# Layer 3's inverse square roots computed on VectorE and GpSimd instead of ScalarE

## The chip, the core and the metric

The kernel runs on one core of one Trainium2 chip. A core has five engines with a queue of instructions each: TensorE (PE, with its weight loads shown as PEld), VectorE (DVE), ScalarE (ACT), GpSimd (POOL) and SyncE (SP, which here only issues transfers). The metric is the device time of one execution in microseconds (us).

## The reference

Four layers follow each other on x of 4 batches x 256 tokens x 256 features, each an attention over a context of 1601 rows and a feed-forward part (ffn), both added to x after a layer norm. The change lies in layer 3:

```python
# L3 attention: 32 heads of 8 dims, 256 queries, 1601 keys per batch
q = x @ Wq.T                      # x: layer-normed tokens, eps 1e-5
k_raw = context @ Wk.T;  v_raw = context @ Wv.T
kv = concat([k_raw, v_raw]).reshape(b, m, NHEADS, HEAD_DIM, 2)   # k, v interleaved
def _rmsnorm(t): return t * rsqrt(mean(t * t, axis=-1) + 1e-6)   # over the 8 dims
q = _rmsnorm(q);  k = _rmsnorm(k)
out = softmax(einsum('bhnd,bhmd->bhnm', q, k) * HEAD_DIM ** -0.5) @ v
x = x + out
# L3 ffn: silu(gate) * up, then down, with activations rounded to 8 bits by their row maximum
x = x + ffn(layernorm(x))
```

Three kinds of inverse square root occur: per key and head (1601 x 32 a batch), per query and head (256 x 32 a batch), and per token (256 a batch) in the two layer norms.

## The kernel before

The program is written in a tile framework: a scheduler fixes the order of instructions on each engine ahead of the run, an engine's queue is worked off strictly in that order, and a tile's buffer is given to its next user when the last reader of the old one is done. Tokens, and keys in tiles of 128 rows (13 tiles, NM = 13), lie on the 128 partitions.

**Keys.** The generator l3_kv(b) makes the keys and values of batch b, one key tile m at a time: a product with the weights wkv into a PSUM bank, one copy to kr (L1683) and two to va (L1685). After m = 4, 9 and 12, l3_squares squares the new tiles into the tile sq3 (one buffer; ScalarE at L1721 where `early()` is true, else GpSimd at L1723) and VectorE sums over the 8 dims into ss (L1724). kr is then multiplied by the inverse roots in ss on GpSimd (L1701, four instructions), transposed on TensorE (L1712), and copied to kT (L1713). Batch 0's keys are made inside layer 2's ffn, where their root is rstd: a Sqrt on ScalarE (L81) and a reciprocal on VectorE (L82). 11 of batch 1's 13 key tiles are made as filling inside queries(0), the list FIRST3 = [7, 1, 3] saying how many at each place; the rest, and batches 2 and 3, beside the attention of the batch before.

**Queries.** queries(b) normalises x (xn, L1767), transposes it (L1797), copies it to xT (L1799), multiplies by wq, copies to qr (L1807), squares (ScalarE) into sqq and sums (L1724), takes the root, multiplies (L1813), transposes (L1824) and copies to qT (L1825). For b > 0 a single Sqrt over 128x482 (L1810) covers the keys (416 columns), the queries (64) and two columns for the token norm of batch b - 2, which the ffn of that batch will use; VectorE's reciprocals follow (L1811 for 66 columns, L1816 twice for 208).

**Norms.** norms(bs) takes mean and variance (L1761, L1762: st, mv) and rstd of the variance into rs.

**Attention.** For every batch 8 groups of heads, and in each 7 pairs of key tiles: scores (s, L77), the exponential on ScalarE (e, L1943), the product with the values (o, L77), where three score tiles (ps_s) may be in flight, and one step of a side generator, beside(b):

```python
for _ in range(NM - 3 if b else NM - sum(FIRST3)):
    next(kv)                       # keys of batch b + 1
    yield
qs = queries(b + 1, st, b - 1 if b else None)
for _ in range(2):
    next(qs)
    yield
for _ in kv: yield                 # multiply, transpose the keys
for _ in qs: yield                 # transpose the queries
...                                # then the ffn of batch b - 1
```

Every side step takes its PSUM bank from bank(), tile b3, of which there is one buffer: the next product into it waits for the copies out of it. After a group of heads os is copied (L2040) and closed (L1960 to L1970: transposed, divided, added to x on GpSimd). spread (L1923) makes the masked queries qb of the next group. The exponential, the Sqrt and the ffn's tanh use different tables of ScalarE; each change of table is an instruction ACT_TABLE_LOAD, shown at the line of the activation that needs it.

Of the kernel before, what the change touches and what calls it, by code (L numbers as in the profile page):

```python
# [11 lines left out]
F32 = mybir.dt.float32  # L12
# [4 lines left out]
I32 = mybir.dt.int32  # L17
AF = mybir.ActivationFunctionType
ALU = mybir.AluOpType
# [39 lines left out]
class Kernel:  # L59
# [19 lines left out]
    def rstd(self, out, in_, scale, eps):  # L79

        self.nc.scalar.activation(out, in_, AF.Sqrt, bias=eps, scale=scale)  # L81
        self.nc.vector.reciprocal(out, out)  # L82

    def layernorm(self, out, x):

# [1582 lines left out]
    def l3_kv(self, b, st, early):  # L1668


        nc = self.nc
        ctxT = self.ctx3
        pool = self.late3 if b % 2 else self.a3
        kr = st["kr"] = self.a3.tile([P, NM, D], F32, name="kr3")
        va = st["va"] = self.va3[b % 2]
        ss = st["ss"] = self.a3.tile([P, (NM + 2) * NH3 + 2], F32, name="ss3")
        for m in range(NM):
            copy = nc.scalar.copy if early() else nc.vector.tensor_copy
            tf = self.take()
            for k in range(2):  # L1680
                self.mm(tf, ctxT[:, k, m * P : (m + 1) * P], self.wkv3[:, k, :], k == 0, k == 1)
            tp = tf.rearrange("p (h d c) -> p h d c", d=HD3, c=2)
            copy(kr[:, m, :].rearrange("p (h d) -> p h d", d=HD3), tp[:, :, :, 0])  # L1683
            for h in range(2):
                copy(  # L1685
                    va[h][:, m, : 16 * (HD3 + 1)].rearrange("p (h e) -> p h e", e=HD3 + 1)[:, :, :HD3],
                    tp[:, h * 16 : (h + 1) * 16, :, 1],
                )
            if m in (4, 9, NM - 1):
                m0 = {4: 0, 9: 5}.get(m, 10)  # L1690
                self.l3_squares(st, kr[:, m0 : m + 1, :], m0, early())
            if m == NM - 1 and b < B - 1:
                self.ctx3 = self.load_ctxT(self.a3, b + 1, 1)
            yield
        if b == 0:
            nk = NM * NH3
            self.rstd(ss[:, :nk], ss[:, :nk], 1.0 / HD3, self.eps6)
        for m0, m1 in ((0, 4), (4, 8), (8, 12), (12, NM)):
            v = kr[:, m0:m1, :].rearrange("p m (h d) -> p (m h) d", d=HD3)
            f = ss[:, m0 * NH3 : m1 * NH3, None].to_broadcast([P, (m1 - m0) * NH3, HD3])  # L1700
            nc.gpsimd.tensor_tensor(v, v, f, ALU.mult)  # L1701
        yield
        yield
        yield
        kT = st["kT"] = [pool.tile([P, MP], F32, name="kT3", bufs=2) for _ in range(2)]
        for m0 in range(0, NM, 4):
            for h in range(2):
                n = min(4, NM - m0)
                copy = nc.scalar.copy if early() else nc.vector.tensor_copy
                tp = self.take().rearrange("p (m k) -> p m k", k=P)  # L1710
                for m in range(n):
                    nc.tensor.transpose(tp[:, m, :], kr[:, m0 + m, h * P : (h + 1) * P], self.ident)  # L1712
                copy(kT[h][:, m0 * P : (m0 + n) * P], tp[:, :n, :].rearrange("p m k -> p (m k)"))  # L1713
                yield

    def l3_squares(self, st, v, m0, early, pool=None):

        n = v.shape[1]
        sq = (pool or self.a3).tile([P, 2 if pool else 5, D], F32, name="sqq3" if pool else "sq3")
        if early:  # L1720
            self.nc.scalar.activation(sq[:, :n, :], v, AF.Square)  # L1721
        else:
            self.nc.gpsimd.tensor_tensor(sq[:, :n, :], v, v, ALU.mult)  # L1723
        self.nc.vector.tensor_reduce(  # L1724
            st["ss"][:, m0 * NH3 : (m0 + n) * NH3], sq[:, :n, :].rearrange("p m (h d) -> p (m h) d", d=HD3),
            AX.X, ALU.add,
        )

    def l3(self, first):

# [10 lines left out]
        with ExitStack() as es:  # L1741
# [30 lines left out]
            def norms(bs):  # L1772

                for b in bs:
                    stats(b)
                v = slice(bs[0], bs[-1] + 1)
                self.rstd(rs[:, v, :], mv[:, v, :, 1], 1.0, self.eps5)

            def queries(b, st, old=None, fill=lambda n: None):

                ss = st["ss"]
                nk, nq = NM * NH3, (NM + 2) * NH3
                if old is not None:
                    stats(old)
                    nc.vector.tensor_scalar(
                        ss[:, nq:], mv[:, old, :, 1], float(HD3), HD3 * (1e-5 - 1e-6), ALU.mult, ALU.add
                    )
                elif b:  # L1790
                    nc.vector.memset(ss[:, nq:], 1.0)
                xn = normed(b, rs[:, b, :])
                fill(0)
                tp = bank().rearrange("p (k q t) -> p k q t", k=2, q=2)
                for k in range(2):
                    for q in range(2):
                        nc.tensor.transpose(tp[:, k, q, :], xn[:, q, k * P : (k + 1) * P], self.ident)  # L1797
                xT = one.tile([P, 2, S], F32, name="xT3")
                nc.vector.tensor_copy(xT, tp.rearrange("p k q t -> p k (q t)"))  # L1799
                fill(1)  # L1800
                yield
                tq = bank().rearrange("p (q d) -> p q d", q=2)
                for q in range(2):
                    for k in range(2):
                        self.mm(tq[:, q, :], xT[:, k, q * P : (q + 1) * P], self.wq3[:, k, :], k == 0, k == 1)
                qr = one.tile([P, 2, D], F32, name="qr3")
                nc.vector.tensor_copy(qr, tq)  # L1807
                self.l3_squares(st, qr, NM, True, one)
                part = ss if b else ss[:, nk:nq]
                nc.scalar.activation(part, part, AF.Sqrt, bias=self.eps6, scale=1.0 / HD3)  # L1810
                nc.vector.reciprocal(ss[:, nk : nq + 2 if b else nq], ss[:, nk : nq + 2 if b else nq])  # L1811
                qrv = qr.rearrange("p q (h d) -> p (q h) d", d=HD3)
                nc.vector.tensor_tensor(qrv, qrv, ss[:, nk:nq, None].to_broadcast([P, 2 * NH3, HD3]), ALU.mult)  # L1813
                if b:
                    for c in range(0, nk, nk // 2):
                        nc.vector.reciprocal(ss[:, c : c + nk // 2], ss[:, c : c + nk // 2])  # L1816
                fill(2)
                yield
                yield
                qT = st["qT"] = two.tile([P, 2, S], F32, name="qT3")  # L1820
                tp = bank().rearrange("p (h t) -> p h t", h=2)
                for h in range(2):
                    for q in range(2):
                        nc.tensor.transpose(tp[:, h, q * P : (q + 1) * P], qr[:, q, h * P : (h + 1) * P], self.ident)  # L1824
                nc.vector.tensor_copy(qT, tp)  # L1825
                yield
# [145 lines left out]
            def beside(b, st):  # L1972

                if b + 1 < B:
                    kv = st["kv"] if b == 0 else self.l3_kv(b + 1, st, lambda: False)
                    if b:
                        for _ in range(3):
                            next(kv)
                            yield
                    if b == 0:  # L1980
                        norms(range(1, B))
                    for _ in range(NM - 3 if b else NM - sum(FIRST3)):
                        next(kv)
                        yield
                    qs = queries(b + 1, st, b - 1 if b else None)
                    for _ in range(2):
                        next(qs)
                        yield
                    for _ in kv:
                        yield  # L1990
                    for _ in qs:
                        yield
                    nq = (NM + 2) * NH3
                    old = [normed(b - 1, st["ss"][:, nq:])] if b else []
                else:
                    for _ in range(3):
                        yield
                    norms([b - 1])
                    old = [normed(b - 1, rs[:, b - 1, :])]
# [12 lines left out]
            kv = second["kv"] = self.l3_kv(1, second, lambda: not busy)  # L2012
            self.l2_add(0)
            norms([0])
            for _ in queries(0, first, None, lambda n: [next(kv) for _ in range(FIRST3[n])]):
                pass
            busy = True
            self.take = bank
# [40 lines left out]
                    :, : 512 if dt is F32 else 1024  # L2059
                ]  # L2060

            norms([B - 1])
            xn = normed(B - 1, rs[:, B - 1, :])
            tail = [ffn(B - 1, q, xn, wide) for q in range(2)]
            while tail:
# [161 lines left out]
```

## Time and profile before

| | |
|---|---|
| median of 6 runs | 2567.95 us (2560.74 to 2572.91) |
| the profiled execution's own time | 2570.77 us |
| its span in the trace | 2568.8 us |
| busy share: TensorE, VectorE, ScalarE, GpSimd | 95%, 55%, 51%, 33% |
| instructions: TensorE, VectorE, ScalarE, GpSimd | 17623, 2915, 3000, 1516 |
| layer 2's ffn and the start of layer 3 | about 1735 to 1941 us |
| attention of batches 0, 1, 2, 3 | 1941 to 2102, to 2265, to 2430, to 2540 us |
| last ffn | 2540 to 2569 us |

All rows come from one profiled execution, so the sums of the prediction start from its own time. A row such as "L1943 ACT ACTIVATE e<-s ... x448 | 404.5, 960 | 159.3 <-PE s L77 154.3" gives line, engine, operation, output and input, count, then busy us and mean ns of one, then the engine's idle time before these and what ended most of it. In a timeline the first two numbers are the start and the length in us; brackets give the idle time ahead and what ended it.

### The profile page before, as it was taken

The page shows a single profiled execution, that of the slowest core. Times are in us where ns is not written, and L with a number is a line of the kernel's source. Part 1 is how long each engine was busy: PE and PEld are TensorE (multiplying, and loading weights), DVE is VectorE, ACT ScalarE, POOL GpSimd, SP SyncE. Part 2 cuts the span into 40 slices and gives each one's busy share as a digit, 9 for nine tenths or more (in the row PEclk, how much of TensorE's full clock was granted, in tenths as well). Part 3 has the DMA queues.
Part 4 walks back from the last instruction along what each step waited for, and adds up shares of the span by engine and source line. Part 5 has one row for each costly group of instructions (what it writes and reads, how often), then busy time and mean ns, then how long its engine had stood idle before and what let it go on. Part 6 is the DMA issues. An engine that isn't in the chain of part 4 may idle for free.

```text
span 2568.8 us, 47102 instructions
## 1 busy us (share of the span) xinstructions
PE 2433.0 (95%) x17623; PEld 1508.6 (59%) x17623; DVE 1408.3 (55%) x2915; ACT 1311.8 (51%) x3000; POOL 840.0 (33%) x1516
## 2 busy tenths in 40 slices
PE   8989987899989999999999999998999999999997
PEld 5778865777645555555555555565554544544553
DVE  5543534843567777777777777763324324334323
ACT  3234444533654545454545454433327766757875
POOL 1015645323345555555555555541011001011000
PEclk9989998989989999999999999998999999999998
DMA  7165574624601111111111111004310100000000
GB/s 252 49 201 169 174 147 149 220 89 140 222 19 48 48 48 48 47 47 48 47 48 48 47 48 47 10 1 176 125 56 28 35 1 28 6 1 2 6 6 5
DMA packets 96474, 188.45 MB, mean 73 GB/s; under 512 B 15401, under 2 KB 64297, under 8 KB 95050
## 3 DMA queue, kind: packets, MB, share of 16 engines
q1 hardware_dynamic: 80102, 146.50, 17.1%
q0 software_dynamic: 10416, 28.46, 4.8%
q10 hardware_dynamic: 5732, 10.49, 1.3%
q8 instruction: 143, 2.34, 0.4%
q14 instruction: 81, 0.66, 0.1%
HBM read 137.29 MB, written 48.11 MB: 72 GB/s over the span
## 4 chain that ended last, share of the span: by engine, by line
PE 84%; DVE 5%; ACT 3%; issue 3%; DMA 2%; POOL 2%; another core or an unknown queue 1%; SPq 0%; ACTq 0%; PEld 0%; POOLq 0%; DVEq 0%; PEldq 0%
PE s L77 25%; PE o L77 24%; PE fill L1241 4%; PE f2gu L77 3%; PE b L77 3%; PE f1gu L77 2%; PE acc L77 2%; PE tpq L77 2%; PE f0gu L77 2%; PE filly L1241 2%; PE tpkv L77 2%; PE av L77 2%; PE f0y L77 2%; PE f2y L77 1%; PE f1y L77 1%
## 5 line engine op out<-in xcount | busy, mean ns | idle before, releaser
L1487 ACT ACTIVATE p<-s,nmsm 128x448 f32<-128x448 f32 (+1 forms) x512 | 326.6, 644 | 382.3 <-PE s L77 247.2
L1943 ACT ACTIVATE e<-s 128x1024 f32<-128x1024 f32 (+1 forms) x448 | 404.5, 960 | 159.3 <-PE s L77 154.3
L77 PE MATMUL o<-pT,va 128*128 128x256 f32 (+2 forms) x1920 | 436.1, 380 | 9.5 <-DVE pT L1528 7.9
L77 PE MATMUL s<-kT,qT 128*32 128x448 f32 (+1 forms) x4096 | 428.9, 559 | 11.2 <-ACT kT L1459 8.2
L77 PEld LDWEIGHTS o<-pT,va 128*128 128x128 f32 (+1 forms) x1920 | 348.9, 192 | 130.9 <-issue 89.6
L1522 POOL TENSOR_SCALAR p<-p,rm 128x448 f32<-128x448 f32 (+1 forms) x512 | 324.4, 655 | 6.2
L1483 DVE TENSOR_REDUCE nmsm<-s 128x2 f32<-128x896 f32 (+1 forms) x256 | 287.5, 1124 | 7.9
L77 PE MATMUL s<-qb,kT 32*128 32x256 f32 (+1 forms) x3328 | 268.1, 405 | 11.0 <-ACT e L1943 11.0
L77 PEld LDWEIGHTS s<-kT,qT 128*32 128x32 f32 x4096 | 120.4, 110 | 265.0 <-issue 240.5
L1528 DVE STREAM_TRANSPOSE pT<-p 128x896 f32<-128x896 f32 (+1 forms) x256 | 270.7, 1112 | 9.4 <-POOL p L1522 8.8
L77 PE MATMUL o<-e,va 128*32 128x256 f32 (+1 forms) x3328 | 236.3, 392 | 1.2 <-DVE os L2040 1.2
L77 PEld LDWEIGHTS s<-qb,kT 32*128 32x128 f32 (+1 forms) x3328 | 163.4, 181 | 105.2 <-issue 75.5
L1515 POOL TENSOR_TENSOR rm<-em,tot 32x8 f32<-32x8 f32 x256 | 54.6, 213 | 402.6 <-DVE tot L1512 391.4
L1241 PE MATMUL fill<-wkc_early,ctxT 128*128 128x256 f32 (+1 forms) x572 | 145.9, 406 | 16.0 <-ACT kT_early L1277 9.7
L1970 POOL TENSOR_TENSOR x<-x,t 128x32 f32<-128x32 f32 x64 | 14.7, 252 | 439.6 <-DVE t L1965 439.6
L77 PEld LDWEIGHTS o<-e,va 128*32 128x32 f32 (+1 forms) x3328 | 90.6, 110 | 115.1 <-issue 75.0
L1480 DVE TENSOR_TENSOR s<-s,mask 128x128 f32<-128x128 f32 (+1 forms) x256 | 84.3, 330 | 107.7 <-PE s L77 95.5
L1241 PEld LDWEIGHTS fill<-wkc_early,ctxT 128*128 128x128 f32 (+1 forms) x572 | 114.5, 204 | 38.0 <-ACT kT_early L1277 11.6
L458 POOL DMA_INDIRECT f0xr<-f0xd,f0src x95 | 90.7, 955 | 67.5 <-PE f0y L77 26.3
L1487 ACT ACTIVATION_READ_ACCUMULATOR p<-s,nmsm 128x1 f32 x512 | 101.7, 199 | 0.0
L77 PE MATMUL f2gu<-f2wgu,f2xsT 128*128 x176 | 83.9, 600 | 0.6 <-ACT f2xsT L74 0.3
L566 POOL DMA_INDIRECT f0yt<-f0yd,f0slot x64 | 63.4, 991 | 60.8 <-DVE x L558 29.7
(488 smaller groups left out, 3506.7 us busy)
## 6 DMA issues: line engine op xcount, KB each, us to landing
ctxT<-in_ctxT SPq DMA_DIRECT2D x9, 1664.0 KB
vd<-va_early SPq DMA_DIRECT2D x96, 128.0 KB
kd<-kT_early SPq DMA_DIRECT2D x48, 256.0 KB
kT<-kd SPq DMA_DIRECT2D x16, 768.0 KB
va<-vd SPq DMA_DIRECT2D x16, 768.0 KB
f0yd<-f0ys SPq DMA_DIRECT2D x95, 128.0 KB
wq<-in_l_wq SPq DMA_DIRECT2D x16, 512.0 KB
wo<-in_l_wo SPq DMA_DIRECT2D x16, 512.0 KB
```

The lines of the kernel that those rows point to most:

```text
L77: self.nc.tensor.matmul(out, lhsT, rhs, start=start, stop=stop, **kw)
L458: nc.gpsimd.indirect_dma_start(out=t, out_offset=None, in_=xd[:, :], in_offset=bass.IndirectOffsetOnAxis(ap=src[:, n : n + 1], axis=0),)
L566: nc.gpsimd.indirect_dma_start(out=yt, out_offset=None, in_=yd[:, :], in_offset=bass.IndirectOffsetOnAxis(ap=slot[:, t, r : r + 1], axis=0),)
L1241: ins = nc.tensor.matmul(tp[:rows, t, :], ctxT[u // NKV2][:, k, c0 : c0 + rows], w[u % NKV2][:, k, :], start=k == 0, stop=k == 1,)
L1480: nc.vector.tensor_tensor(sv, sv, mask[:, 2 * c : 2 * c + 2, : nt - CT, :].rearrange("p n t i -> p n (t i)"), ALU.add)
L1483: nc.vector.tensor_reduce(ms[:, 0, 2 * c : 2 * c + 2], s[:, :, : nt * 32], AX.X, ALU.max, negate=True)
L1487: nc.scalar.activation(p[:, n, : nt * 32], s[:, n, : nt * 32], AF.Exp, bias=ms[:, 0, e : e + 1], accum_out=ms[:, 1, e : e + 1],)
L1515: nc.gpsimd.tensor_tensor(r[32 * a : 32 * a + 32], e[:, a], tot, ALU.mult)
L1522: nc.gpsimd.tensor_scalar(p[:, n, : nt * 32], p[:, n, : nt * 32], r[:, e : e + 1], 1.0, ALU.mult, ALU.mult)
L1528: self.pin(nc.vector.transpose(pT[:, 2 * c : 2 * c + 2, :nt, :].rearrange("p n t i -> p n (t i)"), p[:, :, : nt * 32]))
L1943: nc.scalar.activation(e[:kr, :, :n, :], s[t][:kr, :, :n, :], AF.Exp, scale=1.0 / math.sqrt(HD3))
L1970: nc.gpsimd.tensor_tensor(xt, xt, t[:, q], ALU.add)
```

## The change

A new function root() computes 1/sqrt without ScalarE: a first guess by integer arithmetic on the bits of the number (three VectorE instructions), and three Newton steps. For queries (128x64) and tokens (128x2 each) the steps are on VectorE, three instructions a step, so 12 in all. For keys they are on GpSimd, four instructions a step, in groups of 160, 160 and 96 columns as soon as a group's sums are there; v, y and t lie in the space of the square tile (sq3, or sqq for queries), and the multiplication of kr follows group by group (1280, 1280, 768 columns). All Sqrt of layer 3 but that of the last batch's ffn norm go, with their table loads and reciprocals. The side generator's order becomes: one more step of the key generator, then all of queries(), then the rest of the key generator, then the token norm of the old batch with its own norms().

```diff
+    def root(self, out, in_, scale, eps, space=None, steps=None):
+        vec = self.nc.vector
+        n = in_.shape[1]
+        if space is not None:
+            space = space.rearrange("p m d -> p (m d)")
+            v, y, t = (space[:, k * n : (k + 1) * n] for k in range(3))
+        else:
+            v, y, t = (self.small.tile([P, n], F32, name=f"root_{a}{n}", bufs=2) for a in "vyt")
+        vec.tensor_scalar(v, in_, scale, eps, ALU.mult, ALU.add)
+        yi = y.bitcast(I32)
+        vec.tensor_scalar(yi, v.bitcast(I32), 1, None, ALU.arith_shift_right)
+        vec.tensor_scalar(yi, yi, -1.0, float(0x5F3759DF), ALU.mult, ALU.add)
+        for k in range(3):
+            if steps is None:
+                vec.scalar_tensor_tensor(t, y, -0.5, y, ALU.mult, ALU.mult)
+                vec.tensor_tensor(t, t, v, ALU.mult)
+                vec.scalar_tensor_tensor(out if k == 2 else y, t, 1.5, y, ALU.add, ALU.mult)
+            else:
+                steps.tensor_tensor(t, y, y, ALU.mult)
+                steps.tensor_tensor(t, t, v, ALU.mult)
+                steps.tensor_scalar(t, t, -0.5, 1.5, ALU.mult, ALU.add)
+                steps.tensor_tensor(out if k == 2 else y, t, y, ALU.mult)
...
             if m in (4, 9, NM - 1):
                 m0 = {4: 0, 9: 5}.get(m, 10)
-                self.l3_squares(st, kr[:, m0 : m + 1, :], m0, early())
+                sq = self.l3_squares(st, kr[:, m0 : m + 1, :], m0, early())
+                part = ss[:, m0 * NH3 : (m + 1) * NH3]
+                self.root(part, part, 1.0 / HD3, 1e-6, sq, nc.gpsimd)
+                v = kr[:, m0 : m + 1, :].rearrange("p m (h d) -> p (m h) d", d=HD3)
+                nc.gpsimd.tensor_tensor(
+                    v, v, part[:, :, None].to_broadcast([P, (m + 1 - m0) * NH3, HD3]), ALU.mult
+                )
...
-        if b == 0:
-            nk = NM * NH3
-            self.rstd(ss[:, :nk], ss[:, :nk], 1.0 / HD3, self.eps6)
-        for m0, m1 in ((0, 4), (4, 8), (8, 12), (12, NM)):
-            v = kr[:, m0:m1, :].rearrange("p m (h d) -> p (m h) d", d=HD3)
-            f = ss[:, m0 * NH3 : m1 * NH3, None].to_broadcast([P, (m1 - m0) * NH3, HD3])
-            nc.gpsimd.tensor_tensor(v, v, f, ALU.mult)
...
             def norms(bs):
                 for b in bs:
                     stats(b)
-                v = slice(bs[0], bs[-1] + 1)
-                self.rstd(rs[:, v, :], mv[:, v, :, 1], 1.0, self.eps5)
+                for b in bs:
+                    self.root(rs[:, b, :], mv[:, b, :, 1], 1.0, 1e-5)
...
-                if old is not None:
-                    stats(old)
-                    nc.vector.tensor_scalar(
-                        ss[:, nq:], mv[:, old, :, 1], float(HD3), HD3 * (1e-5 - 1e-6), ALU.mult, ALU.add
-                    )
-                elif b:
-                    nc.vector.memset(ss[:, nq:], 1.0)
...
-                self.l3_squares(st, qr, NM, True, one)
-                part = ss if b else ss[:, nk:nq]
-                nc.scalar.activation(part, part, AF.Sqrt, bias=self.eps6, scale=1.0 / HD3)
-                nc.vector.reciprocal(ss[:, nk : nq + 2 if b else nq], ss[:, nk : nq + 2 if b else nq])
+                sq = self.l3_squares(st, qr, NM, True, one)
+                self.root(ss[:, nk:nq], ss[:, nk:nq], 1.0 / HD3, 1e-6, sq)
...
-                if b:
-                    for c in range(0, nk, nk // 2):
-                        nc.vector.reciprocal(ss[:, c : c + nk // 2], ss[:, c : c + nk // 2])
...
-                    qs = queries(b + 1, st, b - 1 if b else None)
-                    for _ in range(2):
-                        next(qs)
+                    next(kv)
+                    yield
+                    for _ in queries(b + 1, st):
                         yield
                     for _ in kv:
                         yield
-                    for _ in qs:
-                        yield
-                    nq = (NM + 2) * NH3
-                    old = [normed(b - 1, st["ss"][:, nq:])] if b else []
+                    if b:
+                        norms([b - 1])
+                    old = [normed(b - 1, rs[:, b - 1, :])] if b else []
...
-            norms([B - 1])
+            stats(B - 1)
+            self.rstd(rs[:, B - 1, :], mv[:, B - 1, :, 1], 1.0, self.eps5)
```

In the changed file the lines are some 26 further down: the guess is at L95 to L98, the Newton steps at L101 to L103 (VectorE) and L105 to L108 (GpSimd), the multiplication of kr at L1721, the square on ScalarE at L1746, the query transposes at L1836, the exponential at L1955.

## The prediction

> **What bounds the kernel now.** I read the chain of waits first, for what carries the time:
>
> ```profile
> PE 84%; DVE 5%; ACT 3%; issue 3%; DMA 2%; POOL 2%; another core or an unknown queue 1%; SPq 0%; ACTq 0%; PEld 0%; POOLq 0%; DVEq 0%; PEldq 0%
> ```
>
> TensorE sets the end, so an edit counts only by what it takes from or adds to TensorE's idle time. ScalarE's share is 3%, some 77 us over four layers; I ask how much of it is layer 3's roots. Next the table of stretches (TensorE busy, x instructions, then weight loads, VectorE, ScalarE, GpSimd; granted clock; DMA). Its middle three rows are the attention of batches 0, 1 and 2, which make the next batch's keys and queries beside them:
>
> ```profile
> 1735.00:1912.00 177.00, 169.36 (x614) 102.28 (x613) 58.64 (x156) 54.16 (x150) 16.93 (x15) 0.95 0.32 116
> 1912.00:1941.00 29.00, 25.04 (x79) 12.11 (x81) 10.98 (x25) 14.94 (x45) 7.62 (x8) 1.00 0.26 82
> 1941.00:2102.00 161.00, 155.21 (x1928) 82.92 (x1921) 52.92 (x114) 119.77 (x132) 11.84 (x21) 0.98 0.07 25
> 2102.00:2265.00 163.00, 158.96 (x1825) 80.77 (x1823) 58.95 (x143) 106.33 (x120) 16.58 (x23) 0.98 0.04 14
> 2265.00:2430.00 165.00, 159.46 (x1882) 82.39 (x1878) 61.09 (x152) 115.05 (x130) 16.58 (x23) 0.98 0.01 3
> ```
>
> TensorE idles 4 to 6 us in each. The timelines show where: ScalarE, then TensorE, at batch 2's queries.
>
> ```profile
> 2147.34 1.28 ACT L1810 ACT_TABLE_LOAD   x1 [0.80 <-DVE ss L1724]
> 2148.64 0.70 ACT L1810 ACTIVATE ss<-ss,eps 128x482 f32<-128x482 f32 x1
> 2149.35 1.28 ACT L1943 ACT_TABLE_LOAD   x1
> 2150.65 2.85 ACT L1943 ACTIVATE e<-s 128x1024 f32<-128x1024 f32 x3
> ```
> ```profile
> 2147.16 1.13 PE L77 MATMUL s<-qb,kT 32*128 32x256 f32 x8
> 2151.72 2.08 PE L77 MATMUL s<-qb,kT 32*128 32x256 f32 x8 [3.43 <-ACT e L1943]
> ```
>
> The exponentials stop for load, Sqrt, load, and TensorE waits 3.43 us for a score buffer. After it eight score products take 2.08 us, not 1.13: the granted clock is 0.50 for 6.83 us, another 3.4 us lost. Batch 3 repeats that (3.44 us). At batch 1 the gap is 2.65, half clock 3.41: 4.35 in all. After gaps of 1.5, 1.88 and 2.13 us the clock stayed up. So the old roots cost 4.35 + 6.85 + 6.85, plus 1.50 where batch 2's norm takes its Sqrt.
>
> **What goes.** 13 table loads of 1283 ns, 8 Sqrt, some 14 us of VectorE reciprocals. Beside the 19.55 us just listed, the 416-wide Sqrt in layer 2's ffn delays one product round to 4.0 us where 2.8 is regular: -1.15 (B). The norm in front of queries(0) lets ScalarE block 4.29 us and TensorE 2.13; that is in C below.
>
> The Trainium skill ("ScalarE: Activation LUTs", What ACT_TABLE_LOAD costs) puts a switch of tables at 2.66 us, 1.38 of it a drain. Here the exponential starts 0.02 us after a load of 1.28, so I add no drain; by the page's figure, as an estimate, the removed loads would bring 1.38 us more each.
>
> **What comes.** VectorE gets 151 more instructions. A chain of small dependent ones starts every 0.20 to 0.23 us (TENSOR_SCALAR 128x2 170 ns, two-tensor forms 128x64 218 to 225): 12 make 2.5 us at 128x2, 3.0 at 128x64. GpSimd gets 144 Newton operations, whose sizes the trace does not show:
>
> ```profile
> L1442 POOL TENSOR_TENSOR qo<-qo,rq 128x512 f32<-128x512 f32 x32 | 32.6, 1041 | 1.3
> L1515 POOL TENSOR_TENSOR rm<-em,tot 32x8 f32<-32x8 f32 x256 | 54.6, 213 | 402.6 <-DVE tot L1512 391.4
> L1522 POOL TENSOR_SCALAR p<-p,rm 128x448 f32<-128x448 f32 x256 | 160.0, 641 | 6.2
> L1701 POOL TENSOR_TENSOR kr<-kr,ss 128x1024 f32<-128x1024 f32 x12 | 24.2, 2045 | 70.7 <-DVE ss L82 37.5 <-DVE ss L1816 33.2
> ```
>
> A 128x128 product takes 464, so by the line to 512 a 128x160 one takes 0.51, TENSOR_SCALAR 0.40. Three steps of 3 x 0.51 + 0.40 are 5.8 us without gaps, 6.7 with 0.08 us between; I take 6.4 (at 96 columns 5.3). Bounds: 213 ns each (2.6 us) and 0.65 (7.8). GpSimd per batch rises from 6.7 to some 25 us of 163, so its load is no bound; its order is.
>
> (A) Layer 2's ffn starts with GpSimd's gathers of f2xr; group 0's Newton operations stand among the first five. 0 to +3; the gathers were ahead of need, so +0.5.
>
> (C, D) Queries(0) and batch 1. VectorE's token root is 2.5 us for 0.6, its query root 3.0 for 1.04 (Sqrt wait, Sqrt, reciprocal). The first 1.95 is mostly under the fill, which no longer waits 2.13 for ScalarE: +0.4. The second is on the path: +1.95. Thus the first scores come 2.35 later, at 1943.0.
> Then the single sq3 buffer. Newton now works inside it, and ScalarE's Square of batch 1's group 1 needs it; in the changed program that Square stands between the first and second exponential of the attention. Group 0's guess ends at about 1943.7 (its reduction was at 1937.19, moved 2.35, and the guess is behind a copy and residual updates). Newton ends at 1950.1, Square (1.30) at 1951.4, the second exponential at 1952.4, where TensorE has long stopped. VectorE waits too: group 1's reduction 1952.9, its guess among the token roots 1955.1; GpSimd: Newton 1961.5, multiply (2.5) 1964.0, squares of group 2 (1.47) 1965.5; VectorE: its reduction 1966.5, guess 1967.2, and only then the xT copy, 1967.9, for which b<-wq waits. Before, b<-wq began at 1953.87; one more score and value step (2.14) is now ahead of it, so 1956.0 to 1968.0: +12.0, C within it.
> After it the copy, square, reduction, root and multiply (0.69 + 0.63 + 0.69 + 3.0 + 0.63, with hand-overs 6) must pass before the query transposes, and only 3.8 us of scores and values stand between: a stall of 2.2 in place of 4.35 with its clock; the clock is probably down after the 12 us wait, costing 1 to 2. Together -1, so C + D = +11. Bounds: with 213 ns operations two Newtons are 7.6 us shorter (+3.4); with 0.65 it is +14, and with each of some ten VectorE operations waiting 0.4 for GpSimd +18.
>
> (E) Batches 2 and 3, each. The norm of the batch before now sits, with root (2.5), normalisation and quantisation start, ahead of the kr copy of m = 1, and TensorE's next key product needs that copy's bank (one buffer): +2.4. Guesses ahead of the copies: +0.85, +0.6, +0.4. The query stall +2.2. Sum 6.45, against 3.43 and, if no gap exceeds about 2.4, another 3.4 of clock: -0.4 to +3.0, I take +1.4; twice, +2.8.
>
> (F) Last norm: -1.5. The tail keeps its Sqrt: 0.
>
> Moved past at no cost: all of queries() now precedes the rest of the key generator, so the key transposes come later; they need the multiplies, which end group by group (the first long before), and their copies serve the next batch, over 100 us away. GpSimd's residual additions queue behind group 2's Newton (5.3 + 1.6), but their reader, that batch's norm, is a batch away. The context's load on SP stays behind the same copy; no DMA is added.
>
> A rule that speaks against this: VectorE and GpSimd share a port. The row first: a 128x8 operation of VectorE, beside GpSimd's 1.04 us products,
>
> ```profile
> L1440 DVE TENSOR_SCALAR rq<-ss x16: 172/568/577, 685.9 to 1638.6; 128x8 f32<-128x8 f32 x16
> ```
>
> takes 172 ns (minimum) or 568 (median), and xn's 400 becomes 1372 beside the 2.05 us multiplies. So my +18 end above.
> The Trainium skill ("SBUF — State Buffer", Who interferes with whom) calls the pair an exclusive lock held for a whole instruction, also against VectorE operations with two SBUF inputs. By it, estimated, each VectorE step beside a Newton operation could wait one whole operation; Newton's being short, that is 0.5, near the end I have.
>
> Sum: 0.5 - 1.15 + 11 + 2.8 - 1.5 = +11.7. On the profiled execution's 2570.77 that is 2582.4; that execution stands 2.8 above the median, so 2567.95 + 11.7, about 2580.
>
> **The rivals.**
> 1. About even. GpSimd's operations cost some 0.25 us (3 us a group): D falls by about 6.8, E lies at its middle: +5; with the clock kept up in batches 2 and 3 +1. For it: short rows of 213 and 252. Against: 464 at 128 columns.
> 2. Faster. The Square does not wait (VectorE and GpSimd get to group 0 before the exponentials start, so that only C, +2.35, and the query stall, -2.1, are left) and the clock stays up: 0.5 - 1.15 + 0.3 - 0.8 - 1.5 = -2.7; if the query chains of batches 2 and 3 also hide under the scores (-4.4), -7, about 2561. It decides when group 0's Newton ends before about 1945, 1.4 us after I let it start. Against it: 12 operations would need 0.12 us each, below any row; a start 4 us earlier would do.
> 3. Much slower. The port: VectorE's guesses, roots and xn wait behind GpSimd and hold its Newton up in turn, D +18, E +3 each, and the gathers in A +3: about +22, 2590.
>
> **How the numbers follow.** Forecast 0.52 (2573 to 2588), even 0.15, faster 0.15, much slower 0.18. A measurement of this kernel can tell about 0.2%, 5 us, from no change. Faster by more: the faster case's outer half and a little of the even one, 0.14; within: the rest of both and a corner of the forecast, 0.15; slower 0.71. The range leaves out the tails of rivals 2 and 3: 2561 to 2596.
>
> **What would show it.** D: in the changed profile ScalarE idles some 7 us at the Square of sq3 (line 1746) just after the first exponential, waiting for GpSimd, and TensorE's product with wq comes at about 1968. Newton operations of 0.5 us at lines 105 to 108. E: at batches 2 and 3 no 3.43 us gap before s, but gaps before b<-wkv (about 2.4) and before the query transposes at line 1836 (about 2.2), and the clock at 1.0 or 0.5 after them. B and F: a regular 2.8 us round, no gap before the last ffn. It is wrong if Square does not wait, if the Newton operations are near 0.2 or above 0.65, or if TensorE's gaps in 1941 to 2430 sum to less than before.

## The result, and the profile after

The changed kernel takes 2576.46 us (median of 21 runs, 2570.06 to 2582.76), the kernel before 2567.47 on the same chips (42 runs): ratio 1.0032, interval 1.0024 to 1.0041. It is slower by 9.0 us, where 12 were forecast.

The profiled execution of the changed kernel has its own time of 2574.22 us and a span of 2572.5, 3.7 above the span before. That hides something: this execution reached the first transposes of layer 2's gathered rows 6.19 us earlier than the one before did (TensorE's gap ahead of them begins at 1762.41 instead of 1768.60), by work that the change does not touch: at 710 us, before layer 2, it was already 6.18 ahead. From there on it lost 3.7 + 6.19 = 9.9 us, close to the 9.0 of the medians. All differences below are counted from that point.

The ScalarE timeline at the start of the attention, where batch 1's keys are finished:

```profile
1934.67 1.28 ACT L1955 ACT_TABLE_LOAD   x1
1940.67 1.02 ACT L1955 ACTIVATE e<-s 128x1024 f32<-128x1024 f32 x1 [4.72 <-PE s L77]
1944.81 1.27 ACT L1746 ACTIVATE sq<-kr 128x1280 f32<-128x1280 f32 x1 [3.11 <-DVE root_t L102]
1945.99 2.83 ACT L1955 ACTIVATE e<-s 128x1024 f32<-128x1024 f32 x3
```

The Square of group 1 stands between the first and the second exponential and holds ScalarE for 3.11 us. The bracket names VectorE, which at 1944.8 had nothing to do with sq3; the release is the end of GpSimd's Newton (its last operation on sq runs from 1944.26 to 1944.78). Of the 19 table loads from 1735 us on, 6 are left. The description of the kernel gives the ffn's tanh a table of its own; the trace before shows otherwise: twelve tanh (L1890, 2195 to 2464 us) stand among exponentials without a load, so these two share a table, and in the attention only a Sqrt brought loads.

The TensorE timeline of the same stretch (three rows out of it) shows what that becomes:

```profile
1947.05 1.92 PE L77 MATMUL o<-e,va 128*32 128x256 f32 x12 [3.61 <-ACT e L1955]
...
1963.01 3.78 PE L77 MATMUL b<-wq,xT 128*128 128x256 f32 x8 [4.35 <-DVE xT L1816]
...
1972.83 0.66 PE L1836 MATMUL b<-ident,qr 128*128 128x128 f32 x4 [1.46 <-DVE qr L1828]
```

The products with wq take 3.78 us where they took 1.99: the granted clock is 0.50 for 6.83 us from 1960.66. Their row before, which had no gap ahead of it:

```profile
1953.87 1.99 PE L77 MATMUL b<-wq,xT 128*128 128x256 f32 x8
```

The groups of GpSimd's new operations, from 1735 to 2540 us:

```profile
L1721 POOL TENSOR_TENSOR kr<-kr,ss 128x1280 f32<-128x1280 f32 x8 | 19.4, 2430 | 0.6
...
L106 POOL TENSOR_TENSOR sq<-sq 128x160 f32<-128x160 f32 x24 | 13.1, 547 | 1.9
L105 POOL TENSOR_TENSOR sq<-sq 128x160 f32<-128x160 f32 x24 | 11.2, 466 | 96.6 <-DVE sq L98 52.0 <-issue 40.8 <-DVE root_y L103 2.6
...
L107 POOL TENSOR_SCALAR sq<-sq 128x160 f32<-128x160 f32 x24 | 7.9, 331 | 2.0
```

0.47 to 0.55 us for a product; with gaps of some 0.08 the first group takes 6.72 us (1938.06 to 1944.78). In the attention of batches 1 and 2 the 3.43 us gap is gone. The table of stretches, at the bounds used before, and the largest new gap, in the TensorE timeline:

```profile
1941.00:2102.00 161.00, 148.13 (x1841) 79.74 (x1840) 63.92 (x184) 110.13 (x122) 24.85 (x51) 0.96 0.07 25
2102.00:2265.00 163.00, 157.39 (x1825) 80.26 (x1824) 58.80 (x170) 104.02 (x117) 31.36 (x58) 0.99 0.04 14
2265.00:2430.00 165.00, 161.59 (x1909) 83.11 (x1909) 58.24 (x167) 108.87 (x123) 31.38 (x58) 0.99 0.01 3
```
```profile
2100.03 3.20 PE L77 MATMUL b<-wkv,ctxT 128*128 128x512 f32 x4 [2.20 <-DVE va L1711]
```

Between the same bounds as before, batch 0's attention holds 7.1 us less of TensorE work, the next 1.6 less and the one after 2.1 more. In batch 1's, TensorE waits 2.20 us for the key copy behind the old token's root, with 3.41 us of half clock after it, then 1.07 and 0.51 behind guesses, and 1.59 at the query transposes; batch 2's repeats it to 0.01 us.

### The profile page after: what moved, and what is told of

It reads as the page before. It is cut to its first block, busy times and chain, and to the rows that moved or that the text cites. A ratio compares the mean times of both kernels' runs of the same rounds, so it can differ in the third digit from the quotient of the medians.

```text
span 2572.5 us, 47363 instructions
## 1 busy us (share of the span) xinstructions
PE 2432.1 (95%) x17623; PEld 1508.2 (59%) x17623; DVE 1421.9 (55%) x3066; ACT 1292.3 (50%) x2979; POOL 902.0 (35%) x1656
## 5 line engine op out<-in xcount | busy, mean ns | idle before, releaser
L1955 ACT ACTIVATE e<-s 128x1024 f32<-128x1024 f32 (+1 forms) x448 | 404.2, 960 | 177.2 <-PE s L77 171.6
L1267 PEld LDWEIGHTS fill<-wkc_early,ctxT 128*128 128x128 f32 (+1 forms) x572 | 113.8, 202 | 37.0 <-ACT kT_early L1303 16.6
```

Source lines behind the costliest of these rows:

```text
L1267: ins = nc.tensor.matmul(tp[:rows, t, :], ctxT[u // NKV2][:, k, c0 : c0 + rows], w[u % NKV2][:, k, :], start=k == 0, stop=k == 1,)
L1955: nc.scalar.activation(e[:kr, :, :n, :], s[t][:kr, :, :n, :], AF.Exp, scale=1.0 / math.sqrt(HD3))
```

## The experiments

They ran on four other chips, on which the kernel before takes 2522.7 to 2524.1 us, 1.7% less; so runs are compared by their ratio to it on the same chip, and 0.001 is 2.5 us. By the intervals, a difference between two such ratios carries some 4 us of noise. The changed kernel as yardstick:

> The changed kernel itself, as the yardstick on the chip of this call; 0.3% slower than the kernel before, by every theory.

2531.45 us, ratio 1.0034 (1.0022 to 1.0045): +8.

**Undoing one part of batch 1's waits.** `e1_own_space` takes the sq3 buffer out of it, `e2_own_space_sq` GpSimd's queue too:

```diff
-                sq = self.l3_squares(st, kr[:, m0 : m + 1, :], m0, early())
+                spare = kT[m0 // 5][:, : 5 * D].rearrange("p (m d) -> p m d", d=D) if b == 1 and m0 < 10 else None
+                sq = self.l3_squares(st, kr[:, m0 : m + 1, :], m0, early(), sq=spare)     # e2: early() or b == 1
```

> Batch 1's groups 0 and 1 are squared, and their Newton steps worked, in the two still unused kT tiles instead of the one sq3 buffer; nothing else changes. My theory (waits in order, not work): ScalarE's Square of group 1 no longer waits for GpSimd, so the 3.61 us gap at the first values and the half clock after it go; but both reductions and guesses now stand ahead of the qT copy on VectorE (about +2.9 on the first scores), and the product with wq still waits for GpSimd's queue (Newton of both groups, two multiplies, squares: about 23 us from the first guess), so it starts only some 1.5 us earlier. Total -1 to -3 against the changed kernel. Rival 1 (the load on VectorE and GpSimd and their shared port is what costs): no difference, under 1 us. Rival 2 (the single buffer alone makes batch 1's loss): -7.

> As e1_own_space, and batch 1's last group of squares (128x768) on ScalarE, so that GpSimd's queue has nothing that the queries of batch 1 wait for. My theory: the 4.35 us gap at the product with wq goes, and with it the half clock of 6.83 us behind it; ScalarE gets 0.87 us. Total -5 to -8 against the changed kernel, and the first query product about 6 us earlier than in e1_own_space. Rival 1 (load): -1 at most. Rival 2 (single buffer alone): the same as e1_own_space.

e1: 1.0063 (1.0046 to 1.0080), 7 us slower than the changed kernel. e2: 1.0039 (1.0025 to 1.0053), about level with it. e1 lies outside every forecast, e2 outside mine; level is within what rival 1 allowed, but that rival has no place for waits that move, and they did. The gaps at the Square and at wq went; 3.77 us came ahead of the first key product (qT, as expected) and a larger one at the next. e1's TensorE and GpSimd timelines, and three rows of VectorE's:

```profile
1916.72 3.75 PE L77 MATMUL b<-wkv,ctxT 128*128 128x512 f32 x4 [9.88 <-DVE root_t L102]
```
```profile
1909.92 4.77 POOL L1724 TENSOR_TENSOR kr<-kr,ss 128x1280 f32<-128x1280 f32 x2
```
```profile
1910.02 2.33 DVE L103 SCALAR_TENSOR_TENSOR root_y<-root_t,root_y 128x2 f32<-128x2 f32 x1
1912.27 0.15 DVE L102 TENSOR_TENSOR root_t<-root_t,root_v 128x2 f32<-128x2 f32 x1
1912.38 2.33 DVE L101 SCALAR_TENSOR_TENSOR root_t<-root_y 128x2 f32<-128x2 f32 x1
```

Two of VectorE's 128x2 instructions take 2.33 us instead of 0.15: each lies under one of GpSimd's two multiplies and ends with it. Behind them stands the key copy for which TensorE waits 9.88 us. The two steps hold VectorE 4.4 us longer than at 0.15 each; by this estimate 4.4 us of that wait are this blocking, and the rest is mainly what the new order of VectorE's queue costs (reductions and guesses ahead of qT).

**The old token's root.** `e3_norm_rides` writes the old batch's variance beside the query sums, as the kernel before did, and roots 66 columns:

```diff
+                if old is not None:
+                    stats(old)
+                    nc.vector.tensor_scalar(ss[:, nq:], mv[:, old, :, 1], float(HD3), HD3 * (1e-5 - 1e-6), ALU.mult, ALU.add)
...
-                    if b:
-                        norms([b - 1])
```

> The token root of the old batch (batches 0 and 1) is not made alone any more: its variance is written beside the query sums and the query root takes 66 columns, as the Sqrt did before. 24 VectorE instructions fewer; all other roots as changed. My theory: the root, normalisation and quantisation no longer stand ahead of the key copy of m = 1, so in the attention of batches 1 and 2 the 2.20 us gap before the key product and the half clock of 3.41 us after it go: 3.9 each, total -7 to -8. Rival (load): 24 small instructions are 5 us of VectorE at 55% busy, so -1 at most. Rival (generator order): no change, since the order of queries and keys stays.

1.0017 (1.0006 to 1.0028), 4 us better than the changed kernel. The key product of m = 1 follows without a gap and at full clock, 3.9 us gained at each of the two places; the old token's work, now later, gives some of it back in gaps of 1.32 and 0.80 us before the values. The size is half of mine, and the medians alone would allow the load rival's -1; what speaks against it is that the two gaps went where the waits were.

**Batch 0's roots back on ScalarE.** `e4_q0_scalar`: rstd in norms([0]) and in queries(0).

> Only batch 0's token norm and batch 0's query root go back to ScalarE's Sqrt and VectorE's reciprocal; every other root as changed. My theory: the query chain ahead of the first scores is 2 us shorter and the gaps of 0.86 and 1.46 with their half clocks (3.41 us each, 1.7 lost) shrink, the table loads lie under the wait for the layer-2 gathers: -3 to -5.4. Rival (load): 24 instructions fewer, -1 at most. Rival (table loads cost what they last): +1 to +2.6, since two loads come back.

1.0029 (1.0017 to 1.0040), no clear difference to the changed kernel, so the medians decide nothing here. The query chain is shorter, and then ScalarE meets the Square, which now stands ahead of the first exponential and its table load:

```profile
1898.58 1.27 ACT L1746 ACTIVATE sq<-kr 128x1280 f32<-128x1280 f32 x1 [7.74 <-POOL ss L108]
```

7.74 us of waiting for GpSimd, and a TensorE gap of 6.32. What is won ahead of the first group's Newton is lost at it.

**One late root for the keys.** `e5_late_root`: batches 1 to 3 get one 416-column root after the last group, Newton on GpSimd, then four multiplies.

> The keys of batches 1 to 3 get one root of 416 columns after the last group (guess on VectorE, Newton on GpSimd), followed by the four multiplies of the kernel before; batch 0's keys, queries, tokens and the order of the side generator as changed. Waits in order (my theory): ScalarE's Square of group 1 waits only for a reduction, and GpSimd's queue has nothing ahead of the squares of group 2, so the gaps of 3.61 and 4.35 us at batch 1 with their half clocks, and the gaps of 1.07 and 0.51 us behind the guesses of batches 2 and 3, go: -9 to -14 against the changed kernel. Against that, GpSimd's operations (some 0.9 us each) now run beside the query root on VectorE; if each of its 12 steps waits for one of them, that is +5 a batch. Rival (work on VectorE and GpSimd): GpSimd's Newton work falls from 18 to some 10 us a batch, -2 at most.

1.0099 (1.0082 to 1.0116): 16 us slower than the changed kernel. Both of batch 1's first gaps are gone as forecast. The loss is the query root beside GpSimd, for which I had written 5 us a batch. Rows of VectorE's, GpSimd's and TensorE's timelines at batch 2:

```profile
2119.45 0.23 DVE L101 SCALAR_TENSOR_TENSOR sqq<-sqq 128x64 f32<-128x64 f32 x1
2119.71 0.97 DVE L102 TENSOR_TENSOR sqq<-sqq 128x64 f32<-128x64 f32 x1
2120.71 2.00 DVE L103 SCALAR_TENSOR_TENSOR sqq<-sqq 128x64 f32<-128x64 f32 x1
2122.75 1.89 DVE L101 SCALAR_TENSOR_TENSOR sqq<-sqq 128x64 f32<-128x64 f32 x1
2124.67 1.88 DVE L102 TENSOR_TENSOR sqq<-sqq 128x64 f32<-128x64 f32 x1
```
```profile
2120.67 6.38 POOL L1735 TENSOR_TENSOR kr<-kr,ss 128x1024 f32<-128x1024 f32 x4
```
```profile
2128.70 1.11 PE L1845 MATMUL b<-ident,qr 128*128 128x128 f32 x4 [8.79 <-DVE qr L1837]
```

Steps of 0.23 us last as long as a multiply, and the root takes 10.2 us (2117.73 to 2127.92) instead of 3.0.

**Newton steps of the keys on VectorE.** `e6_keys_vector`: no GpSimd argument to root(), so that a group's nine steps run on VectorE.

> The Newton steps of the keys on VectorE (three instructions a step instead of GpSimd's four), in the same groups and places; nothing else changed. Waits in order: a group takes some 3.3 us instead of 6.7, and VectorE's own steps no longer wait for GpSimd's multiplies, so batch 1's two gaps shrink (-4 to -6); in batches 2 and 3 the key copies stand behind a whole root, so the gaps of 1.07 and 0.51 grow by up to 2.5 each (+5 a batch). Total -2 to +6. Rival (GpSimd's slowness and the shared port are the whole loss): -8 or more. Rival (VectorE's load): +3 or more.

1.0086 (1.0069 to 1.0103), 13 us slower than the changed kernel. Batch 1 starts 1.43 us instead of 3.61 late and its wq gap is 1.24, but the key product there waits 4.69, and in batches 2 and 3 the gaps behind the guesses grow from 1.07 and 0.51 to 2.26 and 3.62. That is outside my -2 to +6. That GpSimd's slowness is the whole loss is excluded; the other rival, VectorE's load, had +3 or more and is not excluded by this run, but by e10_best_long below.

**The old order with the new root.** `e7_swapped` is the kernel before with VectorE roots in place of ScalarE's Sqrt for batches 1 to 3, the keys' behind the queries' multiplication, and six ffn steps ahead of the key transposes.

> The kernel before, with only the Sqrt of queries 1 to 3 and of the norms 1 to 3 replaced by VectorE roots: 66 columns for queries and old token first, then one root of 416 columns for the keys, kept behind the multiplication of the queries; token norms of batches 1 to 3 in one root of 6 columns. Batch 0 keeps ScalarE's Sqrt. GpSimd does only squares and multiplies, as before. Six steps of the old batch's ffn (or of the weights) stand ahead of the key transposes, since the multiplies come about 8 us later. By my theory the old stalls (2.65, 3.43, 3.44, 1.5 and the half clocks, 21 us) go and few come back, since no root is on a path that TensorE waits for soon: -10 to -18 against the kernel before. Rival (VectorE's work costs wherever it stands): no gain, within 3 us of the kernel before.

1.0078 (1.0061 to 1.0095): +20 us against the kernel before, against both theories. The four old stalls are gone, and TensorE's timeline at batch 2 has these instead:

```profile
2118.20 0.40 PE L1914 MATMUL b<-idb,xb 128*128 128x128 bf16 x2 [5.22 <-DVE xb L1907]
...
2128.10 1.94 PE L77 MATMUL o<-e,va 128*32 128x256 f32 x16 [4.50 <-DVE os L2085]
```

The scheduler wove the 416-column root between the old token's normalisation (xn, xb), for which the ffn step waits; and the os copy, which frees the only o buffer, stood behind three normalisation instructions of 1.86 to 2.05 us (0.35 to 0.41 otherwise) beside GpSimd's multiplies.

**One Newton step instead of three.**

```diff
-        for k in range(3):
+        for k in range(3 if steps is None else 1):
...
-                steps.tensor_tensor(out if k == 2 else y, t, y, ALU.mult)
+                steps.tensor_tensor(out, t, y, ALU.mult)
```

> The changed kernel with one Newton step for the keys on GpSimd instead of three (the other two are left out, so the keys' roots are rougher); everything else as changed. It takes away two thirds of the suspected cost and no wait's cause: a group's Newton falls from 6.7 to some 2.2 us. If GpSimd's queue at batch 1 carries the loss there, the 3.6 us gap at ScalarE's Square goes, the product with wq starts some 9 us earlier on GpSimd's side, so that its 4.3 us gap goes too, and with them most of two half clocks: -8 to -12 against the changed kernel, that is about level with the kernel before. If the loss is VectorE's roots and the order of the generator, -2 at most.

1.0011 (1.0000 to 1.0022), 6 us better than the changed kernel, a little less than forecast. ScalarE's Square still stands in the way, now ahead of the first exponential, but TensorE loses 1.76 us there for 3.61, and 2.03 at the key product:

```profile
1900.10 1.75 PE L77 MATMUL s<-qb,kT 32*128 32x256 f32 x12 [1.76 <-ACT e L1955]
1905.74 1.96 PE L77 MATMUL b<-wkv,ctxT 128*128 128x512 f32 x4 [2.03 <-DVE root_t L101]
```

There is no gap at wq. Batches 2 and 3 are as in the changed kernel, gap by gap. So the length of GpSimd's Newton at batch 1, and only there, carries some 6 of the 8 us net (2 to 10 by the intervals).

**A version from the runs.** `e9_best`: the kernel before; VectorE roots for batches 1 to 3; queries and old token first, all of queries() ahead of the rest of the keys; the key root held behind them, the transposes six steps later; and a root of eight instructions (one-instruction guess, two steps with tuned constants). In the cut below, the last four lines are shortened.

```diff
+        first = vec.tensor_scalar(v, in_, scale, eps, ALU.mult, ALU.add)
+        if keep:
+            self.tc.keep_in_program_order(first)
+        vec.tensor_scalar(y.bitcast(I32), v.bitcast(I32), -0.5, float(0x5F1FFFF9), ALU.mult, ALU.add)
+        for c, a, z in ((0.703952253, 1.68191391, y), (0.5, 1.5, out)):
+            vec.scalar_tensor_tensor(t, y, -c, y, ALU.mult, ALU.mult)
+            vec.tensor_tensor(t, t, v, ALU.mult)
+            vec.scalar_tensor_tensor(z, t, a, y, ALU.add, ALU.mult)
...
+                    for _ in qs: yield                  # old token's norm, then:
+                    next(more, None); yield             # first ffn step
+                    next(kv); yield                     # key root (keep=True) and multiplies
+                    for _ in range(5): next(more, None); yield
```

> A version put together from the runs. GpSimd makes squares and multiplies alone, as in the kernel before; batch 0 keeps ScalarE's Sqrt; the roots of batches 1 to 3 are on VectorE in eight instructions (guess in one, two Newton steps with tuned constants in the first), queries and old token together (66 columns) right behind the sums, the keys (416 columns) in one root put behind the query and token work, and the key transposes six steps later. No root stands ahead of a copy that TensorE waits for, and no GpSimd operation runs beside the query root. By the theory of waits: the old stalls and half clocks (21 us) go, of which 2 to 6 come back where the qT copy and the old token's normalisation queue up: -12 to -18 against the kernel before. By the theory that the added VectorE work itself costs: within 3 us of it or slower.

0.9949 (0.9935 to 0.9962): 13 us faster than the kernel before, 21 faster than the changed one. The table of stretches over the attention of batches 0 to 2:

```profile
1892.00:2046.00 154.00, 150.04 (x1914) 80.44 (x1910) 58.59 (x135) 111.87 (x125) 14.51 (x21) 1.00 0.08 26
2046.00:2204.00 158.00, 153.88 (x1800) 78.43 (x1793) 57.98 (x153) 103.19 (x117) 16.13 (x23) 1.00 0.04 14
2204.00:2365.00 161.00, 157.43 (x1898) 81.40 (x1896) 62.13 (x174) 108.57 (x124) 16.14 (x23) 1.00 0.01 3
```

The clock stays at 1.00 throughout, and no wait in it exceeds 1.96 us. Two of these waits are of 1.68 us; in e9_again, the same kernel, the clock halved at both.

**Place or length?** `e10_best_long` puts the changed kernel's twelve-instruction root into e9_best's places; `e9_again` is its yardstick.

> As e9_best, with the changed kernel's own twelve-instruction VectorE root (three Newton steps) in place of the eight-instruction one: where the roots stand is the same, only their length differs (query root 3.0 us for some 2.0, key root 6.9 for some 4.6). If the place of the roots is what counts: within 3 us of e9_best, since only the query transposes (gap 0.44) wait for a root, three times a longer one by 1 us: +1 to +4 with the clock. If e9_best's gain came from the shorter root: level with the kernel before, +10 or more against e9_best.

> e9_best once more, on the same chip as e10_best_long, as its yardstick: 0.5% faster than the kernel before, by every theory.

e10_best_long: 0.9984 (0.9975 to 0.9993). e9_again: 0.9949 (0.9936 to 0.9962), on the same chip. The places alone make 4 us against the kernel before, the shorter root another 9; my forecast of 1 to 4 for the length was too small. The query transposes of batches 1 to 3 wait 1.43 to 1.46 us instead of 0.42 to 0.44, the old token's transposes 2.03 and 1.43 instead of 1.24 and 0.64, and batch 1's weights step 1.38 instead of nothing:

```profile
2099.75 0.66 PE L1851 MATMUL b<-ident,qr 128*128 128x128 f32 x4 [1.45 <-DVE qr L1843]
```

All gaps of 0.35 us or more between 1860 and 2490 us sum to 21.7 us in e10_best_long and 14.7 in e9_again.

The same twelve-instruction roots for queries, old tokens and keys stand in e7_swapped in other places; e10_best_long is 24 us faster than that (1.0078 to 0.9984). So the work that is added to VectorE is not the loss by itself; where it stands is.

## Why the prediction was right, point by point

The steps of the sum, each against the same exponential (or fill product) in the two profiled executions:

| step | forecast | measured |
|---|---|---|
| A and B, layer 2's ffn | -0.65 | -0.3 |
| C + D, to batch 1's query transposes | +11 | +12.7 |
| half clock at 2021 us that did not recur | none | -1.6 |
| E, batches 2 and 3 | +2.8 | +1.1 |
| F, last norm | -1.5 | -2.4 |
| tail | 0 | +0.4 |
| sum | +11.7 | +9.9 |

That the sum is off by less than 2 is partly luck: its parts miss by between -1.7 and +1.7 and cancel, and one of them is a half clock that nobody forecast.

D's chain stood as written: the Square between the two exponentials, the second exponential at 1952.5 on the old time scale (1945.99 + 6.52, by which the first norm of layer 3 came earlier) for a forecast 1952.4, wq at 1969.5 for 1968.0. One sign of it was half missed: ScalarE was to idle some 7 us at the Square and idles 3.11, since the first exponential ended only at 1948.2 on that scale and Newton at 1951.3. e8_one_step confirms its cause by taking away two thirds of Newton's length and nothing else. What e1_own_space and e2_own_space_sq correct is the idea behind it that the buffer or the queue could be named as the one cause: with either removed, the next of three late things (Square, key copy, xT) becomes the wait.

C was too small. The first scores came 4.7 us later, not 2.35: the token root is not under the fill. With ScalarE unblocked the fill is done early, and TensorE waits 2.31 us for xn at 1920.45, where I had 0.4. Twice, after this gap and after 0.86 + 1.47 at qr and qT, the clock halves for 3.41 us. In return the wq wait absorbs most of it, so C + D is only 1.7 off.

E's terms: the old token's norm 2.20 for 2.4, guesses 1.07 and 0.51 for 0.85, 0.6 and 0.4, the query stall 1.59 for 2.2. The old stall and half clock went, and the new half clock after the 2.20 is 3.41 and not 6.83: +0.47 and +0.59 for 1.4 each. F was more than its gap: sixteen score products around it took 3.69 us with the 1.50 and take 1.30 now.

The 1.6 us I put down to chance and not to the change: both kernels have a gap of 1.25 us in batch 0's attention (before at 2019.90, after at 2026.13); before, the clock halved after it, after it did not.

The port was priced as a rival; in the changed kernel it does act, once on the path. In its critical chain, between 1906 and 2110 us, stand

```profile
1945.13 2.28 DVE root_y L103
1956.80 2.41 POOL kr L1721
```

a 128x2 step behind which group 1's reduction waits, and the multiply ahead of the squares of group 2. In VectorE's timeline:

```profile
1945.05 2.36 DVE L103 SCALAR_TENSOR_TENSOR root_y<-root_t,root_y 128x2 f32<-128x2 f32 x1
...
1947.40 1.47 DVE L1749 TENSOR_REDUCE ss<-sq 128x160 f32<-128x1280 f32 x1
```

The Square ends at 1946.08, the reduction starts at 1947.40: 1.3 us of D that the prediction had not in its sum. Rival 2, faster, did not come: its condition, a Newton done before 1945 on the old scale, was missed by 6 us. Still open is how the loss of batch 1 divides as a whole between Newton's own length and the blocked VectorE steps; no run takes the blocking away and leaves the length.

Three slips in the working moved nothing that was forecast: the terms of rival 3 add up to 24 and not 22; the attention's rows are the last three of the table of stretches, not the middle three; and GpSimd's 6.7 and 25 us a batch leave out its squares and residual additions (the table's rows have 16.6, and 31.4 after the change).

## What to carry to other kernels

An operation that leaves an engine to free it has to be followed to the queue that it joins: here 8 Sqrt with 13 table loads, worth some 20 us of stalls, became chains, links of which stood ahead of a copy or a buffer that TensorE wanted. Place such chains behind the work that others wait for, hold them there against the scheduler, and shorten them: e9_best gained 4 us by the place and 9 by four instructions fewer. Removing one visible wait tells little until the next late thing is known; two runs that removed the largest gap, e1_own_space and e5_late_root, were slower.

## What the hardware showed beyond expectation

A VectorE instruction can wait for a whole GpSimd instruction: in e7_swapped the 128x256 normalisation did, and so do instructions with two tensor inputs and next to no work. The instruction groups by shape, changed kernel and e5_late_root (min/median/max in ns):

```profile
L103 DVE SCALAR_TENSOR_TENSOR root_y<-root_t,root_y x14: 151/161/2362, 1920.9 to 2422.9; 128x2 f32<-128x2 f32 x14
```
```profile
L103 DVE SCALAR_TENSOR_TENSOR sqq<-sqq x8: 226/738/2003, 1888.8 to 2298.4; 128x64 f32<-128x64 f32 x8
```

The maxima are the lengths of the multiplies (2430 and some 2000 ns). The prediction had only xn's 1372 and an estimate of 0.5 for this. The Trainium skill ("SBUF — State Buffer", Who interferes with whom) says as much of VectorE operations with two SBUF inputs against a GpSimd operation that reads SBUF; these rows agree, and give the price.

The clock changed on a grid. In the changed kernel's layer 3 it halves at 1923.12, 1936.77, 1947.01, 1960.66, 2100.61 and 2264.45 us, all a multiple of 3.41 us apart, for 3.41 or 6.83; the same gap of 1.25 us did it in one execution and not in the other. The Trainium skill ("TensorE: Matmul & The Clock Gate", Part 1) describes a free-running window of that length, which would explain both; that it is the cause is not shown. In the changed kernel both gaps of 2.20 us were followed by 3.41 us of half clock, in e2_own_space_sq neither was. So the price of a gap of 1 to 4 us was 0, 1.7 or 3.4 us in these two kernels, and not by its length alone; a bound from one trace should have kept all three.
